# A four-layer attention and expert kernel on one core: the opening of layer 0 laid out by hand, sort tables made once, zero rows set once, and more buffers for results and early keys

## The chip, the cores and the metric

The kernel runs on one core of one Trainium2 chip. The time is the device time of one execution in microseconds (us), the median over runs. All data are float32. The core has five engines that work side by side: TensorE (PE, matrix multiplies and transposes, with PEld for its weight loads), VectorE (DVE), ScalarE (ACT), GpSimd (POOL) and SyncE (SP), which only issues DMA transfers. Work on different engines is ordered by semaphores, work on one engine by its own order. PE writes to PSUM, a small memory in banks, and the other engines read results from there.

## The reference

Four layers, each a cross-attention of 1024 tokens (4 batches of 256, width 256) to a context of 4 x 1601 rows and a feed-forward part with experts, each added to the running `x`. What matters here, cut down (norms ahead of each part are layer norms without weights):

```python
# layer 0: attention straight on the context, with a mask of the rows that count
scores = einsum('bsd,bmd->bsm', norm(x), ctx) / 16
scores = where(mask[:, None, :], scores, -1e30)
readout = einsum('bsm,bmd->bsd', softmax(scores), ctx)
x += where(any(mask, -1)[:, None, None], readout, 0)
# layer 0, experts: the best 8 of 32, weighted by a softmax over the 8
x += sum over the 8 of  w * (silu(norm(x) @ Wg[e]) * (norm(x) @ Wu[e])) @ Wd[e]
# layer 1: a decaying sum over the context, K = sigmoid(decay), one summary per batch
s_t = K * s_(t-1) + (ctx_t @ W_in + b_in);  summary = mean_t(s_t @ W_out + b_out)
x += norm(norm(x) + summary) * gamma + beta
# layer 1, experts: the best 2 of 8, and shared ones
# layer 2: 16 heads, 4 key heads of 128; keys ctx @ wk_ctx with an RMS norm, values ctx @ wv_ctx
# layer 2, experts: the best 1 of 4;  layer 3: 32 heads of 8, quantised feed-forward
```

In layer 1 the mean over all states turns the scan into one weighted sum of the context rows: the weight of row m is 1 + K + K^2 + ... over the rows that follow it. Neither those weights nor the keys and values of layer 2 depend on `x`.

## The kernel before

The program is written as one long sequence of Python calls. A scheduler orders the instructions of each engine, except those that `keep_in_program_order` (`self.pin`) fixes; tiles come from pools with a number of buffers (`bufs`), and a tile that takes a used buffer waits until the old contents are done with. A tag shares the buffers of a pool among names.

**Opening and layer 0 attention** (`l0_xattn`, 0 to about 140 us of the span). For each batch b and half q of its tokens: `scores` (16 records of PE into four PSUM banks `s0`, of which there is one set), the mask added and the maximum taken on DVE (L260), the exponential on ACT (L268); then `values` of the half before it: 13 transposes of the probabilities `p` through the bank group `tp`, each group copied out by DVE or ACT (L71, L73), and 26 records that sum `av`. All loads go out on SP: `x`, then in turn the transposed context `ctxT` and the plain one `ctxn` of each batch. In front of the first scores stand two side jobs. One finds whether a batch has any valid row: a cast of the whole mask (L207), a reduction `anym` (L209), a small diagonal `anyd` (L211) and a multiply `misc` (L76) that spreads the four flags over the partitions. The other makes the weights of layer 1: a sigmoid, a scan of 1601 steps on one partition (L220), its sum (L224), and five multiplies by a row of ones (L236) that spread the row over 128 partitions, each copied by ACT into `wall` (L238). The reductions `junk` (L314) on DVE multiply the context by it.

**Early work of layer 2** (`l2_early`). Keys and values of 15 of the units (batch, key head) of layer 2 are made ahead of time, in places where PE waits for others. A generator yields 165 steps, and `self.fill(n)` draws n of them. A unit has seven product steps and four turn steps. A product step is four matmuls 128x256 (L76, `fill` or `filly`), two ACT copies into `kr_early` and `va_early` (L1234, L1235) and a write of `va_early` to HBM (L1236). Once a unit's products are done, POOL sets rows 96 to 127 of the last tile of `kr_early` to zero (L1240), ACT and DVE take the norm, and a turn step transposes four tiles (L1262), ACT scales them into `kT_early` (L1264), and SP writes them to HBM (L1265). Steps are drawn in the stages F0 (sort of layer 0, 34 in all), G0 (add of layer 0, 9 x 9), F1 (8), G1 (30) and in the opening of layer 2 (10, and the last 2). The context of unit 4 is loaded (L136) when the generator arrives there, and so on for units 8 and 12.

**Layer 0 experts** (`l0_ffn`). A router, a sort of the 8192 choices by expert on DVE, PE and POOL (140 to 224 us) that needs constant tables (`sort_tables`: a triangle `low`, a mask `keep`, the lane and token numbers), and then a loop over 95 tiles of 128 rows (224 to 385 us): POOL gathers `f0xr` (L433), PE transposes it and multiplies by the expert's weights, and DVE copies the result from PSUM to `f0ys` (L499, three buffers), from which SP writes to `f0yd` in HBM (L500).

**Add of layer 0** (`l0_add`, 385 to 541 us). POOL gathers the eight results of each token back from HBM: 64 indirect DMAs into `f0yt` (L541), 24 buffers. DVE adds them to `x` (L533), and after each second tile the layer 1 attention of that batch follows. Between the tiles nine early steps are drawn; their PSUM tiles alternate between two pools.

Layers 1 to 3 follow in the same manner (layer 1 experts 541 to 690 us, layer 2 attention to 1822, its experts to 2010, layer 3 to the end).

Of the kernel before, what the change touches and what calls it, by code (L numbers as in the profile page):

```python
# [11 lines left out]
F32 = mybir.dt.float32  # L12
BF16 = mybir.dt.bfloat16
U8 = mybir.dt.uint8
# [9 lines left out]
P = 128  # L24
# [34 lines left out]
class Kernel:  # L59
    def __init__(self, ctx, tc, ins, out):  # L60
        self.ctx, self.tc, self.nc = ctx, tc, tc.nc
        self.i, self.out = ins, out
        self.flip = 0
        self.flip4 = False
# [75 lines left out]
    def setup(self):  # L140
# [9 lines left out]
        for b in range(B):  # L150
            t = xp.tile([P, 2, D], F32, name=f"x{b}")
            nc.sync.dma_start(t, i["x"][b].rearrange("(q p) d -> p q d", p=P))
            self.x.append(t)
# [6 lines left out]
        nc.gpsimd.memset(self.eps5, 1e-5)  # L160
        self.eps6 = const.tile([P, 1], F32, name="eps6")
# [3 lines left out]
    def l0_xattn(self):  # L165
        nc, tc, i = self.nc, self.tc, self.i
        with ExitStack() as es:
# [3 lines left out]
            ps = es.enter_context(tc.tile_pool(name="a0p", bufs=2, space=PSUM))  # L171
# [4 lines left out]
            ctxn, ctxT = [], []  # L176
            for b in range(B):
# [8 lines left out]
                ctxT.append(t)  # L186
                t = two.tile([P, NM, D], F32, name="ctxn")
                nc.sync.dma_start(t, i["ctx"][b].rearrange("(m p) d -> p m d", p=P))
                ctxn.append(t)
            self.early = self.l2_early(ctxT)  # L190

            def hidden(b):


                mu = two.tile([P, M], U8, name="mub")
                nc.scalar.dma_start(mu, i["mask"][b : b + 1].to_broadcast([P, M]))
                mf = two.tile([P, M], F32, name="mfb")
                nc.gpsimd.tensor_copy(mf, mu)
                nc.gpsimd.tensor_scalar(mf, mf, -NEG * 16.0, NEG * 16.0, ALU.mult, ALU.add)
                return mf  # L200


            mu = one.tile([B, M], U8, name="mu")
            nc.scalar.dma_start(mu, i["mask"])
            mask = [hidden(0)]
            muf = one.tile([B, M], F32, name="muf", tag="row")
            nc.vector.tensor_copy(muf, mu)  # L207
            anym = one.tile([B, 1], F32, name="anym")
            nc.vector.tensor_reduce(anym, muf, AX.X, ALU.max)  # L209
            anyd = one.tile([B, B], F32, name="anyd")  # L210
            nc.vector.tensor_scalar(anyd, self.ident[:B, :B], anym, None, ALU.mult)  # L211


            dec = one.tile([1, 1], F32, name="dec")
            nc.scalar.dma_start(dec, i["decay"])
            nc.scalar.activation(dec, dec, AF.Sigmoid)
            orow = one.tile([1, M], F32, name="orow", tag="row")
            nc.gpsimd.memset(orow, 1.0)
            wrow = one.tile([1, M], F32, name="wrow")
            nc.vector.tensor_tensor_scan(  # L220
                wrow[:, ::-1], dec.to_broadcast([1, M]), orow, 0.0, ALU.mult, ALU.add
            )
            sw = one.tile([1, 1], F32, name="sw")
            nc.vector.tensor_reduce(sw, wrow, AX.X, ALU.add)  # L224
            misc = ps1.tile([P, 512], F32, name="misc1", tag="misc")
            self.mm(misc[:, 0:B], self.ones[:B, :], anyd, True, True)
            anyb = one.tile([P, B], F32, name="anyb")
            nc.vector.tensor_copy(anyb, misc[:, 0:B])

            def spread_weights():  # L230
                w = one.tile([P, M], F32, name="wall")
                for c0, c1 in (*CC, (M, M + 1)):
                    t = ps1.tile([P, 512], F32, name="misc2", tag="misc")
                    row, to = (sw, self.swb) if c0 == M else (wrow[:, c0:c1], w[:, c0:c1])
                    tc.keep_in_program_order(
                        nc.tensor.matmul(t[:, : c1 - c0], self.ones[:1, :], row, start=True, stop=True)  # L236
                    )
                    nc.scalar.copy(to, t[:, : c1 - c0])  # L238
                return w

            def turned(b):

                xn = self.xn.tile([P, 2, D], F32, name="xn")
                self.layernorm(xn, self.x[b])
# [8 lines left out]
            def scores(b, q, xT):  # L253
                s = ps_s.tile([P, 2048], F32, name="s0")
                for c0, c1 in CC:
                    for k in range(2):
                        self.mm(s[:, c0:c1], xT[:, k, q * P : (q + 1) * P], ctxT[b][:, k, c0:c1], k == 0, k == 1)
# [7 lines left out]
                nc.vector.tensor_scalar(nm, mx[:, 1:2], -1.0 / 16.0, None, ALU.mult)  # L265
                p = two.tile([P, M], F32, name="p0")
                sm = self.small.tile([P, 1], F32, name="sm0")
                nc.scalar.activation(p, s[:, :M], AF.Exp, bias=nm, scale=1.0 / 16.0, accum_out=sm)  # L268
                r = self.small.tile([P, 1], F32, name="r0")
                nc.vector.reciprocal(r, sm)  # L270
                nc.vector.tensor_tensor(r, r, anyb[:, b : b + 1], ALU.mult)
# [27 lines left out]
            last = wall = None  # L299
            xT = turned(0)  # L300
            for b in range(B):
                for q in range(2):
                    now = (b, q, *scores(b, q, xT))
                    if q == 1 and b + 1 < B:
                        xT = turned(b + 1)
                    if q == 0 and b + 1 < B:
                        mask.append(hidden(b + 1))
                    if last is not None:
                        values(*last)
                    if wall is None:  # L310
                        wall = spread_weights()
# [1940 lines left out]
```

## Time and profile before

| | |
|---|---|
| median of 3 runs | 2651.52 us (2648.73 to 2657.36) |
| profiled execution: own time, span | 2653.6 us, 2651.9 us |
| mean granted clock of TensorE | 0.975 |
| PE busy | 2489.8 us, 94% of the span |
| DVE, ACT, POOL busy | 55%, 49%, 28% |
| DMA moved | 186.25 MB, mean 70 GB/s |

The profile is of one execution. Its page gives busy time by engine and in 40 slices, with digits for tenths. A row of a group reads: line, engine, operation, output and inputs, count, then busy time and what ended the idle time before it. In an answer on waits the three figures are us in total, times, and the longest. In a timeline the columns are start, duration, and the instruction, with the idle time of its engine ahead of it in brackets. "issue" is idle time for which the profile shows no releaser. L76 is the line of the helper `mm`, so its groups are told apart by their tiles.

### The profile page before, as it was taken

Reading aid. Unit: us, or ns where it says so; the run is one execution under the profiler, and the core shown is the slowest. Engines: PE = TensorE matmul, PEld = TensorE weight load, DVE = VectorE, ACT = ScalarE, POOL = GpSimd, SP = SyncE. Lnnn points to the kernel's source line nnn. Section 1 sums busy time; section 2 is a strip of 40 time slices with the busy share of each in tenths; the row PEclk is TensorE's granted clock in tenths of the full one; section 3 lists DMA queues with packets and bytes.
Section 4 is the critical chain, followed back from the end, with each engine's and each line's share of the span. In section 5 each row is a group of like instructions: output and inputs, shape, how many; then the busy total and the mean of one; then the engine's idle time right before and its main releaser. Section 6 shows DMA issues by size and latency. Waiting matters only on the chain. (4 is left out here: it accounts for less than half of the span.)

```text
span 2651.9 us, 47069 instructions
## 1 busy us (share of the span) xinstructions
PE 2489.8 (94%) x17800; PEld 1515.1 (57%) x17816; DVE 1471.6 (55%) x3054; ACT 1306.1 (49%) x2973; POOL 746.2 (28%) x1030
## 2 busy tenths in 40 slices
PE   7989986899899999999999999998998999999997
PEld 4678874777545555555555555655564554545553
DVE  6343534753677777777777777774324414233323
ACT  2334443533644445444544444442325775757775
POOL 1014645313334444433443444332102001011000
PEclk8989997999999999999999999998999999999998
DMA  5155574634601111111111110004212100000000
GB/s 201 61 180 151 169 162 150 204 102 153 217 14 46 46 46 46 46 46 46 46 46 46 46 46 21 9 1 155 90 62 66 33 2 27 4 3 2 6 6 5
DMA packets 94656, 186.25 MB, mean 70 GB/s; under 512 B 15053, under 2 KB 62865, under 8 KB 93233
## 3 DMA queue, kind: packets, MB, share of 16 engines
q1 hardware_dynamic: 78278, 144.90, 16.1%
q0 software_dynamic: 10416, 28.46, 4.6%
q10 hardware_dynamic: 5738, 9.87, 1.2%
q8 instruction: 145, 2.38, 0.4%
q14 instruction: 79, 0.64, 0.1%
HBM read 136.77 MB, written 46.42 MB: 69 GB/s over the span
## 5 line engine op out<-in xcount | busy, mean ns | idle before, releaser
L1508 ACT ACTIVATE p<-s,nm 128x448 f32<-128x448 f32 (+1 forms) x512 | 326.5, 644 | 425.1 <-DVE nm L1504 265.1
L1969 ACT ACTIVATE e<-s 128x1024 f32<-128x1024 f32 (+1 forms) x448 | 404.2, 960 | 159.9 <-PE s L76 154.9
L76 PE MATMUL s<-kT,qT 128*32 128x448 f32 (+1 forms) x4096 | 471.9, 558 | 10.0 <-ACT p L1508 5.0
L76 PE MATMUL o<-pT,va 128*128 128x256 f32 (+2 forms) x1920 | 431.0, 376 | 6.0 <-DVE pT L1550 6.0
L1544 POOL TENSOR_SCALAR p<-p,rm 128x448 f32<-128x448 f32 (+1 forms) x512 | 322.5, 652 | 370.9 <-DVE rm L1537 340.6
L76 PEld LDWEIGHTS o<-pT,va 128*128 128x128 f32 (+1 forms) x1920 | 344.4, 191 | 92.9 <-issue 51.4
L1550 DVE STREAM_TRANSPOSE pT<-p 128x896 f32<-128x896 f32 (+1 forms) x256 | 283.8, 1127 | 36.6 <-POOL p L1544 33.0
L1504 DVE TENSOR_REDUCE nm<-s 128x2 f32<-128x896 f32 (+1 forms) x256 | 282.7, 1104 | 3.3
L76 PE MATMUL s<-qb,kT 32*128 32x256 f32 (+1 forms) x3328 | 267.1, 404 | 13.2 <-ACT e L1969 11.0
L76 PEld LDWEIGHTS s<-kT,qT 128*32 128x32 f32 x4096 | 124.0, 110 | 266.3 <-issue 225.2
L76 PE MATMUL o<-e,va 128*32 128x256 f32 (+1 forms) x3328 | 236.1, 392 | 1.3 <-DVE os L2066 1.3
L76 PEld LDWEIGHTS s<-qb,kT 32*128 32x128 f32 (+1 forms) x3328 | 162.6, 181 | 105.8 <-issue 76.2
L76 PEld LDWEIGHTS o<-e,va 128*32 128x32 f32 (+1 forms) x3328 | 90.6, 110 | 115.0 <-issue 74.9
L1996 POOL TENSOR_TENSOR x<-x,t 128x32 f32<-128x32 f32 x64 | 14.7, 250 | 438.6 <-DVE t L1991 438.6
L76 PE MATMUL fill<-wkc_early,ctxT 128*128 128x256 f32 (+1 forms) x532 | 129.2, 393 | 2.8 <-ACT kT_early L1264 2.4
L1501 DVE TENSOR_TENSOR s<-s,mask 128x128 f32<-128x128 f32 (+1 forms) x256 | 83.1, 325 | 69.3 <-PE s L76 64.1
L76 PEld LDWEIGHTS fill<-wkc_early,ctxT 128*128 128x128 f32 (+1 forms) x532 | 103.2, 196 | 20.8 <-ACT kT_early L1264 4.2
L433 POOL DMA_INDIRECT f0xr<-f0xd,f0src x95 | 91.1, 959 | 63.6 <-PE f0gu L76 18.1
L1396 POOL TENSOR_TENSOR qo<-qo,qt 128x512 f32<-128x512 f32 x32 | 41.0, 1283 | 226.0 <-DVE rm L1537 139.6
L1508 ACT ACTIVATION_READ_ACCUMULATOR p<-s,nm 128x1 f32 x512 | 101.7, 199 | 0.0
L76 PE MATMUL f2gu<-f2wgu,f2xsT 128*128 x176 | 84.1, 601 | 0.6 <-ACT f2xsT L73 0.3
L76 PE MATMUL filly<-wkc_early,ctxT 128*128 128x256 f32 (+1 forms) x248 | 67.1, 417 | 13.7 <-ACT kT_early L1264 11.9
(517 smaller groups left out, 3584.1 us busy)
## 6 DMA issues: line engine op xcount, KB each, us to landing
ctxT<-in_ctxT SPq DMA_DIRECT2D x10, 1664.0 KB
f0yd<-f0ys SPq DMA_DIRECT2D x95, 128.0 KB
vd<-va_early SPq DMA_DIRECT2D x90, 128.0 KB
kd<-kT_early SPq DMA_DIRECT2D x45, 256.0 KB
kT<-kd SPq DMA_DIRECT2D x15, 768.0 KB
va<-vd SPq DMA_DIRECT2D x15, 768.0 KB
wq<-in_l_wq SPq DMA_DIRECT2D x16, 512.0 KB
wo<-in_l_wo SPq DMA_DIRECT2D x16, 512.0 KB
```

Of the source, the lines that this page charges most:

```text
L76: self.nc.tensor.matmul(out, lhsT, rhs, start=start, stop=stop, **kw)
L433: nc.gpsimd.indirect_dma_start(out=t, out_offset=None, in_=xd[:, :], in_offset=bass.IndirectOffsetOnAxis(ap=src[:, n : n + 1], axis=0),)
L1396: nc.gpsimd.tensor_tensor(o1, o1, t2, ALU.add)
L1501: nc.vector.tensor_tensor(sv, sv, mask[:, 2 * c : 2 * c + 2, : nt - CT, :].rearrange("p n t i -> p n (t i)"), ALU.add)
L1504: nc.vector.tensor_reduce(nm[:, 2 * c : 2 * c + 2], s[:, :, : nt * 32], AX.X, ALU.max, negate=True)
L1508: nc.scalar.activation(p[:, n, : nt * 32], s[:, n, : nt * 32], AF.Exp, bias=nm[:, e : e + 1], accum_out=sm[:, e : e + 1],)
L1544: nc.gpsimd.tensor_scalar(p[:, n, : nt * 32], p[:, n, : nt * 32], r[:, e : e + 1], 1.0, ALU.mult, ALU.mult)
L1550: nc.vector.transpose(pT[:, 2 * c : 2 * c + 2, :nt, :].rearrange("p n t i -> p n (t i)"), p[:, :, : nt * 32])
L1969: nc.scalar.activation(e[:kr, :, :n, :], s[t][:kr, :, :n, :], AF.Exp, scale=1.0 / math.sqrt(HD3))
L1996: nc.gpsimd.tensor_tensor(xt, xt, t[:, q], ALU.add)
```

## The change

- **The loads of the opening** are put in a new order on SP: `x0`, the mask of batch 0, `ctxT0` in four pieces, `x1` to `x3`, the early weights, `ctxn0`, and then the rest. The masks of the later batches stay on ACT's queue.
- **Norms.** A square root of a constant stands first on ACT. The statistics of batch 0 and the transposes of its tokens come first on DVE and PE; those of batches 1 to 3 are taken together after them (`mv0`, `rs0`); what is made of them is left to the scheduler.
- **The flags of valid rows** are no longer computed: `r` is multiplied by whether the row's maximum exceeds half the masking value.
- **The weights of layer 1** are made by `weights()` after the first maximum: the sigmoid from an exponential, the scan with its result copied (and summed) by ACT, written to HBM as one row and read back over 128 partitions by two DMAs on ACT's queue. The first three `junk` reductions stand together at batch 1.
- **PE's opening**: ten transposes of the identity whose result nobody reads, then the scores of the first half in program order, then three early product steps. Transposes get a third PSUM buffer.
- **Sort tables** for layers 0, 1 and 2 are made once, ahead of everything.
- **Zero rows** of `kr_early`: two tiles are kept for the whole run and their rows are set once.
- **Buffers**: `f0ys` 3 to 6, `f1ys` 3 to 5, `va_early` 6 to 7, `kT_early` 3 to 4, `f0eq` 2 to 1.

The diff, cut to its core:

```diff
+        nc.scalar.activation(const.tile([P, 1], F32, name="root"), self.eps5, AF.Sqrt)
...
-            ps = es.enter_context(tc.tile_pool(name="a0p", bufs=2, space=PSUM))
+            ps = es.enter_context(tc.tile_pool(name="a0p", bufs=3, space=PSUM))
...
+            token(0)
+            nc.scalar.dma_start(dec, i["decay"])
+            hidden(0, nc.sync)
             for b in range(B):
...
+                if b == 0:
+                    for n in range(1, B):
+                        token(n)
+                    self.early = self.l2_early(ctxT)
                 t = two.tile([P, NM, D], F32, name="ctxn")
...
-            muf = one.tile([B, M], F32, name="muf", tag="row")
-            nc.vector.tensor_copy(muf, mu)
...
-                    tc.keep_in_program_order(
-                        nc.tensor.matmul(t[:, : c1 - c0], self.ones[:1, :], row, start=True, stop=True)
...
+            def weights():
+                self.pin(nc.vector.tensor_scalar(dec, dec, 1.0, None, ALU.add))
+                self.pin(nc.vector.reciprocal(dec, dec))
+                wrow = one.tile([1, M + 1], F32, name="wrow", tag="row")
+                self.pin(nc.vector.tensor_tensor_scan(
+                    wrow[:, :M][:, ::-1], dec.to_broadcast([1, M]), self.ones[:1, :1].to_broadcast([1, M]), 0.0,
+                    ALU.mult, ALU.add,
+                ))
+                self.pin(nc.scalar.activation(wall[:1], wrow[:, :M], AF.Copy, accum_out=wrow[:, M:]))
+                wd = self.dram.tile([1, M + 1], F32, name="wrowd")
+                nc.scalar.dma_start(wd, wrow)
+                nc.scalar.dma_start(wall, wd[:, :M].to_broadcast([P, M]))
+                nc.scalar.dma_start(self.swb, wd[:, M:].to_broadcast([P, 1]))
...
-                nc.vector.tensor_tensor(r, r, anyb[:, b : b + 1], ALU.mult)
+                nc.vector.scalar_tensor_tensor(r, mx[:, 1:2], NEG * 8.0, r, ALU.is_gt, ALU.mult)
...
+            t = ps.tile([P, 512], F32, name="idle", tag="tp")
+            for n in range(10):
+                nc.tensor.transpose(t[:, :P], self.ident, self.ident)
+            mv = one.tile([P, B, 2, 2], F32, name="mv0")
+            rs = one.tile([P, B, 2], F32, name="rs0")
+            for b0, b1 in ((0, 1), (1, B)):
+                for b in range(b0, b1):
+                    for q in range(2):
+                        st = self.small.tile([P, 6], F32, name="st0")
+                        self.pin(nc.vector.bn_stats(st, self.x[b][:, q, :]))
+                        self.pin(nc.vector.bn_aggr(mv[:, b, q, :], st))
+                self.rstd(rs[:, b0:b1], mv[:, b0:b1, :, 1], 1.0, self.eps5)
+                if b0 == 0:
+                    xT = turned(0)
+            self.pin(nc.scalar.activation(dec, dec, AF.Exp, scale=-1.0))
...
                     now = (b, q, *scores(b, q, xT))
+                    if last is None:
+                        self.hold = True
+                        self.fill(3)
+                        self.hold = False
...
-                    junk = one.tile([P, M], F32, name="junk0", tag="row")
+                    for c in [] if b == 0 else [(0, 0), (0, 1), (1, 0)] if (b, q) == (1, 0) else [(b, q)]:
+                        junk = one.tile([P, M], F32, name="junk0", tag="row")
...
-            low, keep, lane, tok = self.sort_tables(rt, "f0", E0)
+            low, keep, lane, tok = self.low, self.keep, self.lane, self.tok
...
-                    eq = two.tile([P, K0, E0], F32, name="f0eq")
+                    eq = two.tile([P, K0, E0], F32, name="f0eq", bufs=1)
...
-                ys = two.tile([P, D], F32, name="f0ys", bufs=3)
+                ys = two.tile([P, D], F32, name="f0ys", bufs=6)
...
-                ys = two.tile([P, D], F32, name="f1ys", bufs=3)
+                ys = two.tile([P, D], F32, name="f1ys", bufs=5)
...
+        kept = [e2.tile([P, NM, HD2], F32, name=f"kr_early{n}") for n in range(2)]
+        for t in kept:
+            nc.gpsimd.memset(t[96:, CT2, :], 0.0)
...
-            kr = e2.tile([P, NM, HD2], F32, name="kr_early", bufs=2)
+            kr = kept[u % 2]
...
-                va = e2.tile([P, 2, HD2], F32, name="va_early", bufs=6)
+                va = e2.tile([P, 2, HD2], F32, name="va_early", bufs=7)
...
-                    nc.gpsimd.memset(kr[96:, CT2, :], 0.0)
...
-                kT = e2.tile([P, 4, P], F32, name="kT_early", bufs=3)
+                kT = e2.tile([P, 4, P], F32, name="kT_early", bufs=4)
```

## The prediction

> **What bounds the kernel now.** I read the 40 slices of the page first, to see where TensorE (PE) is short of full. A slice is 66.3 us.
>
> ```profile
> PE   7989986899899999999999999998998999999997
> ...
> PEclk8989997999999999999999999998999999999998
> ```
>
> PE is busy 94% of the span, so time is to be had only where the digits dip: in the first slice (7, clock 8) and in the seventh, 398 to 464 us (6, clock 7). Those are the opening of layer 0 and the add of its expert results. The stretches by time say how deep the dips are (columns: stretch, PE busy, PEld, DVE, ACT, POOL, granted clock, DMA share, GB/s).
>
> ```profile
> 0.00:20.00 20.00, 5.46 (x12) 2.88 (x13) 15.21 (x27) 4.54 (x8) 8.50 (x15) 1.00 0.89 293
> 20.00:40.00 20.00, 18.32 (x36) 7.28 (x35) 10.15 (x21) 5.57 (x9) 0.00 (x0) 0.66 1.00 367
> 40.00:60.00 20.00, 17.39 (x81) 12.24 (x80) 18.25 (x29) 3.12 (x5) 4.50 (x2) 1.00 0.01 1
> ...
> 350.00:400.00 50.00, 41.08 (x218) 33.12 (x217) 15.25 (x44) 21.50 (x73) 18.50 (x20) 1.00 0.83 170
> 400.00:500.00 100.00, 67.93 (x291) 55.36 (x290) 49.03 (x116) 38.71 (x109) 56.28 (x61) 0.81 0.55 171
> ```
>
> In the first 20 us DVE, not PE, is full; from 20 to 40 PE is busy but at a clock of 0.66. The waits of PE and its timeline in the opening name both:
>
> ```profile
> PE misc L76 <- DVE anyd L211: 12.4, 1, 12.4
> ```
>
> ```profile
> 16.25 7.29 PE L76 MATMUL s<-ctxT,xT 128*128 128x512 f32 x16 [0.68 <-ACT xT L250]
> ...
> 35.37 6.25 PE L76 MATMUL s<-ctxT,xT 128*128 128x512 f32 x12
> ...
> 49.40 5.71 PE L76 MATMUL s<-ctxT,xT 128*128 128x512 f32 x16
> ```
>
> PE starts at 12.36 on a mask reduction that only the last multiply needs; a set of 16 score records costs 7.29 us, then some 10.4 with the weight-row spreads between, and 5.71 at full clock. At 49.40 the third set, scores(1,0), starts; after that the loop has its period (15.0, then 13.7 us). So 49.40 is the mark of the opening.
>
> In the add stage (385 to 541) PE waits 36.6 us in all, among them:
>
> ```profile
> PE filly L76 <- ACT kT_early L1264: 11.3, 3, 6.8
> PE fill L1262 <- issue: 8.7, 2, 6.4
> PE filly L1262 <- issue: 6.5, 1, 6.5
> PE filly L1262 <- ACT va_early L1235: 4.5, 3, 2.6
> ```
>
> The waits of POOL and, at the end of the expert loop, of DVE:
>
> ```profile
> POOL kr_early L1240 <- PE fill L1262: 17.6, 3, 14.3
> POOL kr_early L1240 <- PE filly L1262: 13.2, 2, 9.1
> ```
>
> ```profile
> DVE f0ys L499 <- DMA f0yd<-f0ys: 14.8, 8, 3.7
> ```
>
> **What the Trainium skill says.** "TensorE: Matmul & The Clock Gate", Part 1, has PE at half rate until it has been busy for some 3.4 us and again after an idle window of that length. The trace agrees: 0.66 in 20 to 40, 0.60 in 400 to 430 us. "ScalarE: Activation LUTs", section What ACT_TABLE_LOAD costs, gives 1283 ns for any set; the opening shows three loads of 1.28 us. "DMA: Bandwidth & Descriptors", section Issuing engines are not separate DMA queues, says that all queues share 16 engines; here the loads of the opening run at 293 to 367 GB/s and end by 40 us whoever issues them, so an order can only choose which comes first.
>
> **The change, part by part.** Own time of the profiled execution 2653.6 us (span 2651.9); the median of three runs is 2651.5, 2.1 less, inside their spread of 2648.7 to 2657.4.
>
> *Opening.* Removed from DVE: the cast of the mask (0.98), anym (1.79), anyd (2.17), the reduce of the row (1.80). Removed from PE: the misc matmul and the spreads of the weight row, seven matmuls, about 6.8 us of PE at the clock of that time. Removed from ACT: a table load (sqrt's comes at once). In the changed instruction order x0 is the first load on SP, then the mask, then ctxT0. x0's bn_stats began at 3.74 before, though it had to wait for nothing but its load; then 0.43+0.16+0.38+0.17 for the statistics, 0.29 sqrt, 0.15 reciprocal, two of 0.5 for xn: 6.4. Transposes 1.12, xT copy 0.58: 8.1. Before, the same copy ended at 16.20. ctxT0 (1664 KB behind 256 and 200 KB) needs 7.2 us at 293 GB/s and its last chunk is due near 12: not late. Ten idle transposes hold the clock up, so scores 5.7 (7.3 if they fail): 13.8. Three early product steps, 8 matmul records each, which last 1.89 us in the timeline: 5.4, to 19.2, covering the mask add (2.05) and the exp (1.60) that free the scores' PSUM. scores(0,1) 5.7: 24.9. Transposes of x1 0.66, values(0,0) 8.05 as in the timeline (41.35 to 49.40): 33.6. The mark moves from 49.4 to 33.6; I take **-15.5**, from -11 (half clock in both score sets, ctxn0 or wkc 3 us late, since by 20 us some 5 MB must have come) to -18. The mask's 200 KB now pass on SP ahead of ctxT0 (0.7 us at that rate, in the 7.2), and x1 to x3 pass behind it; their statistics are due only at 24.9. A third PSUM buffer for transposes replaces the bank of the spreads. Moved at no cost by my count: the weight row now goes through HBM on ACT's queue (scan 3.45, a copy of 1601 of about 1.6, write, broadcast). ACT stands behind that write's landing; the first x load of 256 KB took 2.9 us from issue to use, so 2 to 4 us, between 21.5 and 25, under scores(0,1). Behind it wait the copy of xT(1) and the exp of (0,1): both due at 25 or later. If that cover goes, 2 to 4 us are lost. The junk reductions (1.83 each) need the row and stand at b=1, where DVE had two of them late before too.
>
> *Early steps.* Of 165 steps, three are now made in time that PE would have waited; later stages hold 3 less. Those are 5.4 us of product time where PE is the bound, but at the very end of the sequence, in the opening of layer 2, three turns of 0.6 us and the gaps around them: **-4** (-1 to -6).
>
> *Expert loop of layer 0.* f0ys from 3 to 6 buffers. From 350 to 400 PE lost 8.9 of 50 us, where 250 to 350 lost 1.9 per 50; 1.6 of it lies after 385. So 5.4 is the most that the 14.8 us of DVE waits cost the end; the gathers of f0xr share the DMA engines and stay slow (PE waits there for f0xr as well): **-4** (0 to -8). f0eq from 2 to 1 buffers: one PE gap of 1 us shows it before, 0 to +1.
>
> *Add of layer 0.* The memset of kr per unit goes (15 on POOL become 2). It held POOL for 36.5 us in all while gathers queued behind it. va_early gets a seventh buffer, kT_early a fourth, and the load of ctxT for unit 4, issued at 387 amid writes and gathers, now comes three steps earlier, before the expert loop. PE's waits that name kT_early or va_early are 11.3+4.5+1.8+1.2+1.0 = 19.8 of the 36.6; half of that is **-9**. The rest shows "issue" while gathers run. Late next: the f0yt gathers themselves, 64 of 0.95+0.30 = 80 us, and DVE's adds that free their 24 buffers. Bounds: all waits gone, -37; or more stall, see the rivals.
>
> *Elsewhere.* Tables of the sorts (a few POOL instructions before each sort; the last set, 1822.5 to 1823.7, ran beside DVE and PE): 0, now about 2 us on POOL ahead of mfb, which was ready 3 us before its use; f1ys 3 to 5 and the rest: **-1** (+1 to -3).
>
> Sum: -15.5-4-4-9-1 = -33.5, so 2653.6-33.5 = 2620; against the median 2618. I say **2619**.
>
> **Rivals.**
> 1. *Only the opening pays.* The stalls among the gathers and the slow end of the expert loop are those of the DMA engines (share 0.83) and take no notice of buffers: -15.5-4 = 2634. For it: half of PE's waits name no buffer.
> 2. *The add stage runs through.* With POOL never parked and the big load out of the way, 25 to 30 of the 36.6 us go: 2598 to 2604. For it: PE's work there is 119 us of 156. Against: 24 buffers and DVE's adds.
> 3. *The opening waits for data.* ctxn0 stands behind x1 to x3, wkc and ctxT0; if its use waits, the opening gives 7 and the sum is 2628.
> 4. *Slower: gathers without a break stall PE.* Place: 402.2 to 423.5 us, where POOL issues 13 gathers end to end and PE stands idle for 6.48+6.39+6.78 = 19.65, 1.51 us per gather. Before, the memset broke up the later bursts. If the other 40 past the first 24 now stall PE at that price, 60 us replace the 15 they cost: +45, and with the 24.5 gained elsewhere the kernel ends at 2674. It decides from about +33 on, 1.2 us per gather. Against: DVE's adds pace those gathers.
> 5. *No change*: the opening is given back to the same stalls, +15 to +30 there: 2645 to 2659.
>
> **How the numbers follow.** Forecast (2608 to 2630, case 3 in it) 0.52; rival 1 (to 2641) 0.2; rival 2 0.14; rival 5 0.08; rival 4 0.06. About 0.3%, 8 us, is what a measurement of this kernel can tell: same is 2644 to 2660. Faster 0.87, same 0.08, slower 0.05. The range leaves out the far end of rival 2 and most of 4 and 5: 2598 to 2642.
>
> **What would show it.** Right: xT's copy ends near 8, scores(1,0) start near 33.6 (wrong over 40); clock 0.9 or more in 10 to 30; no DVE wait of f0ys on its DMA; PE's waits in the add stage under 30 us; no POOL wait on PE there. Wrong: a wait of PE on ctxn or wkc before 30 us, ACT's exp of (0,1) behind the row's write, or PE idle over 45 us in the add stage.

## The result and the profile after

The changed kernel takes **2629.22 us** (median of 6 runs, 2623.32 to 2633.99), the kernel before 2650.85 on the same chip (6 runs): a ratio of **0.9913, 95% interval 0.9897 to 0.9929**, 21.6 us. The forecast was 2619 in 2598 to 2642. The profiled execution has a span of 2627.3 us (own time 2629.0), 24.6 less than before.

The lines that answer to those shown of before. The slices of the page:

```profile
PE   8989977999899999999999999998998999999997
...
PEclk9999998999999999999999999998999999999998
```

The first slice rose from 7 to 8, and the dip is now at the sixth and seventh (7, 7): it has moved with the add stage, not filled up. The stretches by time:

```profile
0.00:20.00 20.00, 15.02 (x43) 8.96 (x44) 8.92 (x30) 4.80 (x9) 5.63 (x24) 1.00 0.88 288
20.00:40.00 20.00, 18.81 (x79) 12.98 (x78) 11.04 (x21) 7.69 (x14) 3.05 (x2) 1.00 1.04 399
40.00:60.00 20.00, 18.25 (x84) 12.37 (x83) 12.63 (x22) 6.42 (x10) 4.71 (x2) 1.00 0.38 110
...
350.00:400.00 50.00, 31.87 (x155) 24.89 (x153) 8.99 (x23) 14.18 (x45) 25.04 (x27) 0.86 0.60 149
400.00:500.00 100.00, 85.48 (x382) 70.97 (x382) 68.64 (x162) 51.31 (x144) 39.79 (x41) 0.90 0.58 181
```

PE is busy 15.0 of the first 20 us where it was busy 5.5. The waits of PE from 0 to 60 us, and its timeline there:

```profile
PE tp_ln L245 <- DVE xn L239: 1.9, 1, 1.9
PE av L77 <- DVE pt L72: 1.9, 3, 1.1
PE idle L306 <- POOL eps L159: 1.5, 1, 1.5
PE s L254 <- DMA ctxT<-in_ctxT: 1.5, 1, 1.5
```

```profile
8.60 8.85 PE L254 MATMUL s<-ctxT,xT 128*128 128x512 f32 x16 [1.52 <-DMA ctxT<-in_ctxT]
17.29 5.40 PE L1241 MATMUL fill<-wkc_early,ctxT 128*128 128x256 f32 x24
22.52 5.71 PE L254 MATMUL s<-ctxT,xT 128*128 128x512 f32 x16
...
33.27 1.13 PE L254 MATMUL s<-ctxT,xT 128*128 128x512 f32 x2 [0.58 <-ACT p L271]
...
38.13 4.85 PE L254 MATMUL s<-ctxT,xT 128*128 128x512 f32 x14
...
50.73 5.71 PE L254 MATMUL s<-ctxT,xT 128*128 128x512 f32 x16
```

The wait of 12.4 us is gone. The first 16 score records took 8.85 us where 5.71 is full speed, though the clock column shows 1.00: it has no record of a lower clock there, the lengths of the records do. Two records of scores(1,0) stand at 33.27, ahead of 18 of the `av` records, and the other 14 follow at 38.13. The next full set, scores(1,1), starts at 50.73; it stood at 64.40 before.

The waits of PE in the add stage (columns: total, times, longest), then those of POOL there:

```profile
PE fill L1241 <- issue: 7.7, 2, 7.4
PE filly L1275 <- ACT va_early L1249: 6.7, 5, 2.8
PE filly L1241 <- ACT kT_early L1277: 5.6, 2, 5.4
PE fill L1275 <- ACT va_early L1249: 3.1, 3, 2.7
```

```profile
POOL f0yt L566 <- DVE x L558: 36.7, 13, 12.7
```

POOL no longer waits on PE, and PE waits nearly as long as before: from the last `f0ys` to the first gather of layer 1 its idle time sums to 35.0 us, 38.5 before. The 14.8 us that DVE waited for `f0yd` before `f0ys` have no line any more.

### The profile page after: what moved, and what is told of

The parts are those of the page before. It is cut to its first block, busy times and chain, and to the rows that moved or that the text cites. A ratio compares the mean times of both kernels' runs of the same rounds, so it can differ in the third digit from the quotient of the medians.

```text
span 2627.3 us, 47055 instructions
## 1 busy us (share of the span) xinstructions
PE 2488.6 (95%) x17798; PEld 1518.7 (58%) x17814; DVE 1459.8 (56%) x3041; ACT 1303.6 (50%) x2968; POOL 746.6 (28%) x1002
## 4 chain that ended last, share of the span: by engine, by line
PE 82%; DVE 6%; ACT 4%; issue 3%; DMA 2%; POOL 2%; another core or an unknown queue 1%; SPq 0%; ACTq 0%; PEld 0%; POOLq 0%; PEldq 0%; DVEq 0%
PE s L77 25%; PE o L77 22%; PE fill L1241 3%; PE f2gu L77 3%; PE b L77 3%; PE tpkv L77 2%; PE f1gu L77 2%; PE f0gu L77 2%; PE filly L1241 2%; PE av L77 2%; PE acc L77 2%; PE f0y L77 2%; PE f2y L77 1%; PE tpq L77 1%; POOL p L1557 1%
## 5 line engine op out<-in xcount | busy, mean ns | idle before, releaser
L1241 PE MATMUL fill<-wkc_early,ctxT 128*128 128x256 f32 (+1 forms) x520 | 134.4, 410 | 11.3 <-issue 7.9
L2009 POOL TENSOR_TENSOR x<-x,t 128x32 f32<-128x32 f32 x64 | 14.7, 250 | 439.9 <-DVE t L2004 439.9
L1514 DVE TENSOR_TENSOR s<-s,mask 128x128 f32<-128x128 f32 (+1 forms) x256 | 83.2, 325 | 77.5 <-PE s L77 72.7
L566 POOL DMA_INDIRECT f0yt<-f0yd,f0slot x64 | 62.4, 975 | 67.6 <-DVE x L558 36.7
## 6 DMA issues: line engine op xcount, KB each, us to landing
f0yd<-f0ys SPq DMA_DIRECT2D x95, 128.0 KB
vd<-va_early SPq DMA_DIRECT2D x90, 128.0 KB
```

The lines of the kernel that those rows point to most:

```text
L566: nc.gpsimd.indirect_dma_start(out=yt, out_offset=None, in_=yd[:, :], in_offset=bass.IndirectOffsetOnAxis(ap=slot[:, t, r : r + 1], axis=0),)
L1241: ins = nc.tensor.matmul(tp[:rows, t, :], ctxT[u // NKV2][:, k, c0 : c0 + rows], w[u % NKV2][:, k, :], start=k == 0, stop=k == 1,)
L1514: nc.vector.tensor_tensor(sv, sv, mask[:, 2 * c : 2 * c + 2, : nt - CT, :].rearrange("p n t i -> p n (t i)"), ALU.add)
L2009: nc.gpsimd.tensor_tensor(xt, xt, t[:, q], ALU.add)
```

## Where the time went, stage by stage

The runs came to several chips, which fall into two kinds. On kind A (the chip of the result above, and those numbered 0 and 9) the kernel before takes 2651 to 2652 us, on kind B (numbers 6 and 7) 2614 to 2615. So totals are compared as ratios to the kernel before as measured beside them on the same chip. On B the first three experiments below ran on chip 6, the other three on chip 7; their kernels before differ by 0.5 us. From each trace the same marks: end of layer 0's attention (last add of `x` from `av`), first gather `f0xr`, first and last `f0ys`, first gather `f1xr`, last `f1ys`, first scores of layer 2. The column "add" runs from the last `f0ys` to the first `f1xr`, so it takes in layer 1's router and sort behind the stretch from 385 to 541. Differences of these starts in us, worked out from one profiled execution each; the stage between first `f1xr` and last `f1ys` is 68.4 in all of them and left out. The last column, all after the first scores of layer 2, moves between 1936 and 1944 without a pattern: so far do single executions differ.

| kernel, kind of chip | opening and attention | sort | to first f0ys | expert loop | add | to layer 2 | after |
|---|---|---|---|---|---|---|---|
| before, A | 140.8 | 78.0 | 13.3 | 152.5 | 193.6 | 66.4 | 1938.9 |
| changed, A | 128.6 | 72.6 | 15.4 | 149.5 | 193.5 | 62.2 | 1937.1 |
| before, B | 143.2 | 79.7 | 11.3 | 143.1 | 163.3 | 66.3 | 1939.2 |
| changed, B | 128.5 | 72.6 | 15.8 | 140.6 | 151.1 | 62.2 | 1939.8 |
| opening only, B | 128.5 | 76.2 | 15.8 | 141.8 | 159.8 | 66.8 | 1941.6 |
| all but the opening, B | 141.6 | 79.4 | 12.1 | 140.4 | 151.7 | 66.0 | 1940.6 |
| kT_early 3, B | 129.1 | 75.3 | 15.4 | 141.2 | 152.9 | 62.5 | 1942.2 |
| zero rows per unit, B | 128.8 | 74.3 | 15.7 | 140.5 | 161.0 | 61.8 | 1936.5 |
| plain loads, B | 129.1 | 72.7 | 15.5 | 141.0 | 150.9 | 62.6 | 1943.3 |
| plain loads, A | 128.0 | 74.3 | 15.4 | 149.9 | 151.1 | 62.8 | 1936.4 |
| va_early 6, A | 128.5 | 74.7 | 14.7 | 149.1 | 190.4 | 62.8 | 1943.5 |
| no early steps, A | 129.8 | 67.4 | 12.5 | 150.4 | 192.3 | 66.6 | 1935.7 |
| more idle transposes, A | 131.6 | 74.3 | 14.4 | 149.6 | 193.7 | 62.3 | 1936.6 |
| the same, load spread, A | 131.1 | 72.6 | 11.0 | 152.5 | 188.8 | 62.3 | 1943.2 |

## The experiments

**The opening alone.** The changed kernel with

```diff
-                ys = two.tile([P, D], F32, name="f0ys", bufs=6)
+                ys = two.tile([P, D], F32, name="f0ys", bufs=3)
...
-        for t in kept:
-            nc.gpsimd.memset(t[96:, CT2, :], 0.0)
...
+                    nc.gpsimd.memset(kr[96:, CT2, :], 0.0)
```

and likewise `f1ys` 3, `va_early` 6, `kT_early` 3, `f0eq` 2. The early steps and the tables made once stay with the opening.

> The changed kernel with f0ys, f1ys, va_early, kT_early and f0eq at their old counts and the zero rows set per unit again; only the opening, the three early steps and the tables made once stay. Theory A (the sort of layer 0 ran 5.4 us shorter because kT_early has a fourth buffer, and the expert loop 3.0 us because of f0ys): sort stage, last av to first gather f0xr, 78 us as before; expert loop, first to last f0ys, 152 us; in all 8 us above the changed kernel, 2637. Rival B (the shift of three early steps moved the turns off the places where PE waits; buffers give nothing): sort stage 73 us, expert loop 149, in all 2629 to 2631. Both: opening 12 to 13 us shorter than before at the last av.

Measured: ratio 0.9952 (0.9935 to 0.9969), on B: 12.4 us of 2614.5. Attention 14.7 shorter, sort 3.5, first tiles 4.5 longer, add 3.5 shorter. The opening, with the early steps and the tables, is worth some 12 us. Theory A would leave 8 us to the buffers and zero rows; on B (below) the changed kernel is another 20 us faster than this one. Rival B, to whom they give nothing, fails as well: the sort stands at 76.2 us here and at 72.6 with them.

**kT_early back at three buffers.**

```diff
-                kT = e2.tile([P, 4, P], F32, name="kT_early", bufs=4)
+                kT = e2.tile([P, 4, P], F32, name="kT_early", bufs=3)
```

> The changed kernel with kT_early back at 3 buffers. Theory A: PE waits named kT_early in the sort stage come back (2 to 7 us), the stage takes 77 to 79 us for 73, in all 2633 to 2635. Rival B: 73 us and 2629, within 2 us.

Measured: ratio 0.9908 (0.9890 to 0.9925). It ran on B, and the totals expected were for A, so they mean nothing here. Against the changed kernel on B (below) it is 7.3 us above by the medians, of which the sort shows 2.7 and the add 1.8. But the two ran on different chips, and their intervals overlap (0.9890 to 0.9925, 0.9850 to 0.9899): it is likely, not shown, that the fourth buffer helps.

**Plain loads in place of the gathers of the add, first time.**

```diff
-                nc.gpsimd.indirect_dma_start(
-                    out=yt, out_offset=None, in_=yd[:, :],
-                    in_offset=bass.IndirectOffsetOnAxis(ap=slot[:, t, r : r + 1], axis=0),
-                )
+                nc.sync.dma_start(yt, yd[(t * K0 + r) * P : (t * K0 + r + 1) * P, :])
```

> The changed kernel with the 64 gathers f0yt of the add of layer 0 replaced by 64 plain loads of as many rows in their stored order, on SP: the rows added are not those of the token, the bytes and the work after them are the same. Theory D (PE's stalls there, 36 us, come with the gathers made by POOL): PE waits between the last f0ys and the first f1xr fall under 15 us and the kernel to 2600 to 2610. Rival E (they come with the traffic on the DMA engines, reads and writes alike): PE waits stay at 30 us or more and the time within 5 us of 2629, or above it, since the loads now stand in SP's queue among the writes of keys and values.

The rows added are then not those of the token, so this serves to measure only. Measured: ratio 0.9884 (0.9856 to 0.9911), add stage 150.9 us. On B the changed kernel itself takes 151.1 there: on B the gathers cost nothing, and what they cost on A stayed open.

**Both kernels again, on B.** No edit.

> The kernel before once more, for its trace on the chip of the other runs here: the opening-only and kT_early runs came from a chip on which the kernel before takes 2614 us, 37 less than where it was first profiled, and their add stage took 153 to 160 us against 193.5 in both first traces. Theory F (the long PE stalls of that stage belong to the chip of the first traces, not to either kernel): add stage, last f0ys to first f1xr, 155 to 165 us here too. Rival (the stalls vary from execution to execution): 190 or so again in some of the runs of this call.

> The changed kernel once more, on the same chip as the kernel before. Theory G (opening 12, buffers and zero rows 10 of which most in the two add stages, nothing from f0ys and kT_early): 22 to 25 us under before, add stage 150 to 154 us, 7 under that of before; sort stage within 1.5 us of before's less the shift of early steps. Rival A (kT_early and f0ys pay on every chip): sort stage 5 us and expert loop 3 us shorter than in the kernel before on this chip.

Measured: before 2615.00 us (median of 11 runs; the profiled one took 2616.17), changed 2582.31, ratio **0.9874 (0.9850 to 0.9899)**, 32.7 us. Theory F holds: 163.3 and 151.1 us for the add stage. Theory G had the length of the changed kernel's add stage right, but the gain there (12.2) and the total are larger than it says. In the sort and the loop its rival A comes nearer: they are 7.1 and 2.5 us shorter than before on B, too. The waits of PE in the add stage, of the kernel before and then of the changed one:

```profile
PE fill L76 <- ACT kT_early L1264: 8.6, 5, 7.2
PE filly L1262 <- ACT va_early L1235: 2.4, 1, 2.4
```

```profile
PE tp_ln L127 <- DVE xn L95: 2.0, 1, 2.0
PE fill L1241 <- ACT kT_early L1277: 1.5, 4, 0.7
```

Where the long stalls of A are absent, one wait of 7.2 us stands in the kernel before, and the change takes it away.

**All but the opening.** The kernel before with zero rows set once, `va_early` 7, `f0ys` 6, `f1ys` 5, `f0eq` 1. A fourth `kT_early` does not fit beside the old opening: the pool `a0` would need 71.3 KB per partition, and 70.6 are left. So `kT_early` stays at 3, and the table `f0lane16` moves to a pool that closes after the sort.

> The kernel before with zero rows set once, va_early 7, f0ys 6, f1ys 5, f0eq 1 (and the 2 KB table of the sort in a pool that closes early, for room); kT_early stays 3, the opening stays. Theory G: 9 to 11 us under before, add stage 7 shorter, layer 1 add 4 shorter. Rival H (the buffers pay only behind the shifted early steps, since the load of ctxT for unit 4 still stands amid the writes): 0 to 4 us under before, add stage as before.

Measured: ratio 0.9954 (0.9938 to 0.9969), 12.5 us; add stage 151.7, that is 11.6 shorter than before and more than theory G expects; the stretch to layer 2, where it expects 4 us, is unchanged (66.0). Rival H fails: the buffers and zero rows pay without the early steps. With the 12.4 of the opening that makes 24.9 of 32.7. What both kernels lack is the fourth `kT_early`; the 7.3 measured without it, on another chip, would fill the gap.

**Zero rows per unit again, va_early 6**, the rest as changed.

```diff
                 elif m == NM - 1:
+                    nc.gpsimd.memset(kr[96:, CT2, :], 0.0)
```

> The changed kernel with the zero rows set per unit again on POOL and va_early at 6; f0ys, f1ys, kT_early as changed. Theory G1 (the memset on POOL, which waits for PE and holds the gathers, is what costs): add stage 158 to 160 us, 6 to 8 us above the changed kernel in all; layer 1 add as the changed kernel. Rival G2 (f0ys and f1ys carry the 10 us): within 2 us of the changed kernel.

Measured: 2589.19 us, ratio 0.9900 (0.9874 to 0.9927), 6.9 us above the changed kernel on the same chip (2586.06 to 2592.65 against 2580.66 to 2583.13); add stage 161.0 for 151.1. Theory G1's size, but not its mechanism. The timeline of the first burst of gathers (start, duration, instruction, idle time before it):

```profile
393.01 0.94 POOL L566 DMA_INDIRECT f0yt<-f0yd,f0slot  x1 [0.30 <-issue]
393.95 0.23 POOL L1254 MEMSET kr_early<- 32x128 f32 x1
394.21 0.31 ACT L1260 ACTIVATE sq_early<-kr_early 128x128 f32<-128x128 f32 x1 [8.96 <-POOL kr_early L1254]
...
395.15 1.22 PE L1241 MATMUL fill<-wkc_early,ctxT 128*128 128x256 f32 x2 [7.85 <-ACT kT_early L1278]
```

In this burst the memset does not hold up the gathers. It stands behind them on POOL; ACT's square stands behind the memset for 8.96 us, the scaling of `kT_early` behind the square, and PE behind that for 7.85. Elsewhere in the stage POOL does stand at the memset, 38.9 us in all, but no other wait of PE there is longer than 2.0 us.

**va_early back at six**, alone.

> The changed kernel with va_early back at 6 buffers alone; zero rows set once. With the zero rows set per unit as well, the add stage took 161 us against 151 and the kernel 7 us more. Theory J1 (the memset on POOL makes the 7.85 us stall in the first burst of gathers): stage 151 to 153, kernel within 2 us of the changed one. Rival J2 (it was the seventh buffer, which lets a unit's seven writes go out without a wait): stage 159 to 161, 6 to 8 us above the changed one.

Measured: ratio 0.9922 (0.9897 to 0.9947), add stage 190.4 us. It ran on A, where the stage takes 188 to 194 us in every kernel that gathers there. No loss is seen, but A would hide one. That the memset and not the buffer made the 10 us rests on the timeline above, which shows 7.85 of them.

**More idle transposes**: 17 for 10, and 8 between the transposes of x0 and the first scores.

```diff
-            for n in range(10):
-                nc.tensor.transpose(t[:, :P], self.ident, self.ident)
+            for n in range(17):
+                self.pin(nc.tensor.transpose(t[:, :P], self.ident, self.ident))
...
+                    for n in range(8):
+                        self.pin(nc.tensor.transpose(t[:, :P], xn[:, 0, :P], self.ident))
```

> The changed kernel with 17 idle transposes for 10 and 8 more between the transposes of x0 and the first scores, all in program order. Theory I (the first scores ran 6 us of their 8.85 at half clock because PE had been idle from 3.9 to 5.85 and from 7.1 to 8.6): scores(0,0) take 5.7 to 6.5 us, the second set of batch 1 starts 2 to 3 us earlier, and the kernel is 2 to 3 us under the changed one. Rival (ctxT0's chunks arrive at that pace): scores(0,0) end at 17 as before, nothing gained.

Measured: ratio 0.9918 (0.9893 to 0.9943), attention 3.0 us longer, not shorter. PE's timeline, then DVE's:

```profile
8.76 5.78 PE L260 MATMUL s<-ctxT,xT 128*128 128x512 f32 x16 [1.25 <-DMA ctxT<-in_ctxT]
...
21.93 5.81 PE L260 MATMUL s<-ctxT,xT 128*128 128x512 f32 x16 [1.57 <-ACT p L277]
```

```profile
16.47 1.38 DVE L239 TENSOR_SCALAR xn<-x,mv,rs 128x256 f32<-128x256 f32 x4
17.77 1.22 DVE L267 CUSTOM_DVE_ANT_0 s<-s,mfb 128x1024 f32<-128x1024 f32 x1
```

The half clock was the cause of the 8.85 us: the set now takes 5.78. But the mask add still starts at 17.77 (17.61 in the changed kernel), since DVE first does the statistics of x1 to x3, which land at 12.6, and their norms. The next set must wait for the exponential, PE falls idle for 1.57 us, and the time is lost again further on: the 18 `av` records after two records of scores(1,0) take 5.74 us where they took 4.05.

**The early steps left out of the opening.**

```diff
-                        self.fill(3)
+                        pass
```

> The changed kernel without the three early steps in the opening; they are made later, as before. Theory K (the three steps give 5 us of work in waiting time, -3.5 in the sort and -4 in the opening of layer 2, but let the scheduler put the 1664 KB load of unit 8's context right ahead of the expert loop, +4.5 at its first tiles): opening about 2 us shorter at the last av, sort stage 76 us, first gather to first f0ys 11 to 12, layer 1 add to first scores of layer 2 66 us; in all 2 to 5 us above the changed kernel. Rival (the shift is worth the full product time wherever PE is the bound): 5 us or more above.

Measured: ratio 0.9898 (0.9875 to 0.9921) against 0.9913, so no loss is seen where both theories had it slower. Layer 2's opening is 4.4 us longer and the first tiles 2.9 shorter, as theory K has it, but the sort is 5.2 *shorter*. The stretches of the sort in the changed kernel, then without the steps:

```profile
128.00:148.00 20.00, 16.87 (x91) 14.30 (x89) 12.74 (x60) 6.43 (x19) 3.79 (x5) 0.91 0.51 160
148.00:168.00 20.00, 16.79 (x74) 13.62 (x75) 9.00 (x25) 11.32 (x27) 4.46 (x6) 0.91 0.91 300
168.00:188.00 20.00, 19.74 (x95) 16.01 (x95) 9.86 (x21) 6.29 (x18) 0.15 (x1) 0.91 0.53 164
```

```profile
130.00:150.00 20.00, 16.93 (x101) 15.03 (x100) 12.00 (x59) 6.56 (x18) 1.18 (x2) 1.00 0.65 197
150.00:170.00 20.00, 17.37 (x84) 14.02 (x83) 10.24 (x31) 11.98 (x30) 6.79 (x8) 1.00 0.70 224
170.00:190.00 20.00, 20.00 (x106) 17.01 (x105) 9.42 (x20) 6.60 (x19) 0.00 (x0) 1.00 0.73 248
```

PE is as busy in both, but at a clock of 0.91 in the changed kernel, so it gets fewer records done (91, 74, 95 against 101, 84, 106). In three spells of 3.4 us its clock is 0.5, which costs 5.1 us (an estimate, half of 10.2), as much as the stages differ by. Without the steps there is no such spell, though the same number of early records runs in the stage. Why the steps bring the spells is not shown.

**The load of ctxT spread over the loop**, on top of the idle transposes: four pieces behind the writes of tiles 8, 14, 20 and 26, in program order.

```diff
+                if n in (8, 14, 20, 26):
+                    self.late((n - 8) // 6 * 416)
```

> As the run with more idle transposes, and the load of ctxT that the scheduler put ahead of the expert loop is cut into four pieces that stand in program order behind the writes of tiles 8, 14, 20 and 26. Theory K: first gather to first f0ys 11 to 12 us for 15.8, the rest of the loop no more than 1 us longer, the kernel 3 to 4 us under the run with idle transposes and 5 to 7 under the changed one. Rival (the wait at the first tiles is of the first gathers themselves): first f0ys unchanged, no gain.

Measured: ratio 0.9929 (0.9903 to 0.9955). First `f0ys` after 11.0 us for 14.4, so the load was what the first tiles waited for; the loop then takes 152.5 for 149.6. The load costs about 3 us in either place.

**Plain loads again**, the edit as above.

> The changed kernel with plain loads of rows in stored order on SP for the 64 gathers of the add of layer 0, a second time: the first time it came to a chip on which neither kernel stalls there, and told nothing. If this chip takes 2650 us for the kernel before: theory D (the 20 us of PE stalls in the first burst come with the gathers that POOL makes) add stage 150 to 165 us for 193.5, PE waits there under 10 us, the kernel 28 to 40 us under the changed one (ratio to before 0.976 to 0.981). Rival E (the stalls come with any traffic on that chip): stage over 180 us, PE waits over 20. If the chip takes 2615 us: as the first time, ratio 0.988, and the question stays open.

Measured, on A: ratio **0.9765 (0.9743 to 0.9787)**, add stage 151.1 us where the changed kernel takes 193.5. PE's waits in that stage, then the stretch of the first loads and, of the changed kernel on A, that of its first burst of gathers:

```profile
PE tp_ln L127 <- DVE xn L95: 2.0, 1, 2.0
PE fill L1238 <- ACT kT_early L1274: 1.5, 4, 0.7
```

```profile
365.00:395.00 30.00, 30.00 (x154) 25.66 (x153) 12.41 (x27) 19.54 (x52) 0.00 (x0) 1.00 0.78 244
```

```profile
370.00:400.00 30.00, 13.82 (x59) 10.71 (x57) 2.34 (x4) 6.13 (x17) 22.58 (x24) 0.77 0.50 150
```

PE is busy throughout, with more bytes moved (244 GB/s for 150). The stalls on A do not come with traffic as such; they come with the gathers that POOL makes. Theory D holds. The edit changes two things at once, who issues the transfers and that rows are read in stored order; which of them matters is not separated.

The traces show more of how the stall looks. The same four transposes of PE and ACT's scaling of their result, in the changed kernel on A and then on B:

```profile
377.93 0.60 PE L1275 MATMUL fill<-ident,kr_early 128*128 128x128 f32 x4
392.43 0.69 ACT L1277 ACTIVATE kT_early<-fill,kw_early 128x512 f32<-128x512 f32 x1 [7.24 <-remote]
```

```profile
369.28 0.60 PE L1275 MATMUL fill<-ident,kr_early 128*128 128x128 f32 x4
369.99 0.70 ACT L1277 ACTIVATE kT_early<-fill,kw_early 128x512 f32<-128x512 f32 x1
```

On B the scaling follows 0.7 us after the transposes begin, on A 14.5. It waits for PE's semaphore ("remote" is a wait whose releaser the view does not name), and the update that lets it go is recorded at 392.40, 6.7 us after the end of PE's last record before it. So while PE waits for ACT, ACT waits for a signal of PE. In the add stage of the changed kernel on A, 31 of PE's 123 signals have no update on record within 1 us of the end of their matmul, and in the expert loop, where POOL gathers too, 54 of 371. On B there is none in either, and with plain loads on A none in the add stage.

## Why the prediction came out as it did

The sum was -33.5 us against the profiled execution; that execution lost 24.6, and the medians 21.6. On B the medians lost 32.7. By its terms, for the traces of A:

- **Opening, -15.5.** -12.2, inside the bounds of -11 to -18. The term that was mis-sized is the path to the second set of scores, 19.2 us in the sum and 22.52 in the trace. The first scores were given 5.7 us and took 8.85 at half clock, the case priced at 7.3: the ten transposes end at 3.9 us, PE idles twice before the scores, and the scores start at 8.60 for 8.1. A full clock alone would have brought the second set only 0.6 us forward, as the run with more idle transposes shows (21.93), since a second limit lies right behind: the sum let the mask add follow the scores at 13.8, with the statistics of x1 to x3 "due only at 24.9", but these and their norms hold DVE from 12.41 on, and the mask add starts at 17.61. The mark was badly chosen, too: 33.27 looks like the 33.6 forecast, but only because two records of the set were put ahead of 18 `av` records; the next set shows 13.7 gained. The weight row's write took 4.7 us, longer than the 2 to 4 estimated. ACT's line is

```profile
31.05 0.58 ACT L247 COPY xT<-tp_ln 128x512 f32<-128x512 f32 x1 [4.59 <-DMA wrowd<-wrow]
```

and the exponential behind it starts at 31.53, 0.3 us after its maximum (`nm`, 31.07 to 31.22) had been made: the cover held, with nothing to spare. Two readings of the prediction are high, without weight for the sum: DVE, called full, is busy 15.2 of the first 20 us, and the matmuls taken off PE last 6.3 us in the timeline of before, not 6.8.
- **Early steps, -4.** The gain came where it was forecast and was lost elsewhere. Without the steps the marks give 4.4 back at layer 2's opening and 1.2 at the attention, and gain 5.2 in the sort and 2.9 at the first tiles: 2.5 us to the steps' debit, in one execution each. The step that failed priced the moved work at full clock and looked only at where it was taken from. The load of ctxT (the context of units 8 to 11, loaded when the steps reach unit 4; the prediction calls it unit 4's) is issued at 205.2 in the changed kernel and at 362.5 without the steps (387.0 before), so it is the steps that bring it ahead of the loop. By the count of steps, the products of units 0 to 3, which read what stood in its buffer before, are done after 36; with the three in the opening 37 are drawn ahead of the loop, without them 34. I saw that move and counted it only as a gain for the add stage.
- **Expert loop, -4.** -3.0, and 2.1 given back at its first tiles; the waits on `f0yd` are gone as forecast. On B, where six buffers against three can be compared only in kernels that differ in more than that, it is 0.6 us with the new opening (141.8 and 141.2) and 2.7 with the old (143.1 and 140.4).
- **Add of layer 0, -9.** Nothing on A (193.6, 193.5), -12.2 on B. The sign named for it, waits of PE under 30 us, failed on A. The step that failed took the waits that name `kT_early` and `va_early` for waits on buffers. With the gathers gone from POOL they vanish in a kernel that has the same buffers, so on A they were stalls that come with the gathers: at the place that rival 4 gives, and taking no notice of buffers, as rival 1 has it. Rival 1's cause, the load on the DMA engines, falls with the plain loads (share 0.78, no stall). Rival 4's growth did not occur: 35.0 us of idle PE for 38.5. And the memset was read the wrong way round: I priced the 36.5 us that POOL stood with it, and the trace with zero rows per unit on B shows the cost in its standing behind a burst of gathers.
- **The sort, no term.** -5.4, which the prediction did not have. In the trace of before PE waits 2.34 and 4.78 us there for `kT_early`, and 13.6 us run at half clock. Without the early steps but with the fourth buffer the stage takes 67.4 for 78.0. I added up such waits for the add stage alone.
- **Elsewhere, -1.** -4.2 between the last `f1ys` and layer 2. It returns without the early steps (66.6), so it is the gain that was priced under them. The opening alone, which has the steps but the old buffers, keeps 66.8, so it takes the steps and the buffers together. `kT_early`, `va_early` and the zero rows are not the buffers in question (61.8 to 62.8 without them); `f1ys` is left as the likely one, not tested alone.

So rival 1's number (2634) is nearest on A, and the forecast's on B. That the total came out within the range on A is luck: an unpriced gain in the sort stood in for an expected one in the add. On B, too, the sum is met in part by the sort, which gains 7.1 us against 4.5 lost at the first tiles, neither with a term of its own.

What stays open: why signals come late while POOL gathers on A and not on B; and how much of the add's gain on B the seventh `va_early` carries. That a kernel without the early steps beats the changed one is not shown, since the intervals overlap (0.9875 to 0.9921, 0.9897 to 0.9929) and they were not measured side by side.

## What to carry to other kernels

When a wait names a buffer, look at what stands ahead of the releasing instruction on its own engine before adding buffers: here a 0.2 us memset behind a burst of gathers made a 7.85 us stall on PE, two engines away. Work moved into an idle place is worth what it takes away later at the clock that runs there, and it also moves what was ordered behind it; compare the stages at both ends. A price taken from one chip's trace for a stall without a named releaser should carry the whole stall as its range, and where the releaser is an engine, look whether that engine was itself waiting for a signal.

## What the runs showed of the hardware

- Chips differ in two stages of the same program in which POOL gathers: the add of layer 0 by 30 to 42 us (before 193.6 and 163.3, changed 193.5 and 151.1) and the expert loop by 9 (152.5 and 143.1, 149.5 and 140.6). With plain loads in the add both kinds take 151 us there, and the loop, which still gathers, keeps its 9 (149.9 and 141.0). The stages of layer 1 that gather are as long on both (68.4; 66.4 and 66.3). On the slower kind signals between engines come late in the two stages, 6.7 us in the case shown above.
- PE's clock: in the changed kernel, beside gaps of 2.58 and 1.80 us in the sort, spells of 3.4 us at 0.5 appear; a gap of 1.79 in the kernel without the early steps has none, and a third spell had no gap of over 0.7 us within 10 us ahead of it. The Trainium skill, "TensorE: Matmul & The Clock Gate", Part 1, gives an idle window of some 3.4 us as the condition; the spells' length agrees with that, the gaps here were shorter. So were those of the kernel before ahead of its 0.66 in 20 to 40 us: from PE's first record at 12.36 to the spell's start at 26.1 none is over 1.51 us, so that figure shows the half rate but not the condition.
- A write of one row of 6.4 KB to HBM on ACT's queue was issued at 25.45, and the transfer on that queue that reads it back, which waits for it, at 30.17: 4.7 us, in a stretch that moved 399 GB/s.
